# Second expert products two steps behind the first, groups of at most two tiles, and another order of the last jobs, in a two-layer graph network

## The chip, the cores and the metric

The kernel runs on one core of a Trainium2 chip. Its time is the device time of one execution, in microseconds (us). The kernel before takes 2432.77 us, the median of three runs (2429.38 to 2436.04).

## The reference

The network has 3125 nodes with 256 features each and 103125 edges, sorted by destination. It has two layers, and x is carried through both. Cut to what matters here:

```python
xn = layernorm(x)
x = x + edge_conv_max(xn, src, dst) + attention0(xn)          # layer 0
x = x + moe0(layernorm(x))
xn = layernorm(x)                                             # layer 1
h_all = einsum('ni,rio->nro', xn, W)                          # 8 relations
agg = segment_sum(h_all[src, edge_type], dst)
h = gelu(agg + xn @ loop_w + h_bias + xn)
x = x + layernorm(h) * ln_gamma + ln_beta + attention1(xn)
xn = layernorm(layernorm(x)) * gamma + beta                   # experts of layer 1
logits = xn @ Wr + br                                         # the two largest: softmax -> w
for e in range(8):
    y = y + w[:, e] * (gelu(xn @ W1[e] + b1[e]) @ W2[e] + b2[e])    # 256 -> 512 -> 256
x = x + y
```

All eight experts are computed for every node, and w is zero for six of them. Everything is in 32-bit floats. The change lies in layer 1, from `segment_sum` to the end.

## The kernel before, in words

The nodes are sorted by their number of incoming edges and lie in 25 tiles of 128 rows; the last one, tile 24, has 53. The table `STEPS` says how many rows a node of a tile needs at most: 45 for tile 0, 43 for tile 1, 38 for tile 4, 36 for tile 6, 24 for tile 23 and 22 for tile 24. One gather (an indirect DMA issued by POOL, line 195) fetches one row for each of the 128 nodes of a tile, so a tile takes as many gathers as its number in `STEPS`.

**Second layer, gathers.** `edge_pass` (L1336) goes through groups of tiles. The rows of a tile come in chunks of up to four gathers into a buffer `gt` from a pool of five (`gp1`, L2013). DVE adds the rows of a chunk together (L1376) and to the tile's sum `acc` (L1378). A gather into a buffer can start once the additions on the chunk that used it five chunks ago are done. The out rows are scattered by POOL (`flush`, L242) only after the last gather. The groups stand in `GROUPS1` (L67 to 69): tiles (3,4), (1,2), (23,24), (19 to 22), (15 to 18), (12 to 14), (9 to 11), (7,8), (6), (5), (0). The first two pairs have a pass of their own, `first_groups`.

**Second layer, jobs.** When a group's sums are complete, `after1` (L2544) puts its further work into a list `bg` of jobs with costs. After each chunk, `edge_pass` works out a rate, the sum of the costs in `bg` divided by the gathers left in the group, held between 0.9 and 1.3; each gather gives so much credit, and jobs are taken from the list as long as there is credit:

```python
rate = min(max(sum(c for c, _ in bg) / left, pace[0]), pace[1])
credit = min(credit, 0.0) + rate * n1 if bg else 0.0
while bg and credit > 0.0:
    cost, job = bg.popleft()
    job()
    credit -= cost
```

So the order of the program decides which jobs lie between which chunks. DVE and POOL do their work in the order in which it is written; the order on TensorE (PE) and ACT is found by a planner from that.

**A group's jobs** (class `Group`, L2315). *First jobs:* the self loop and attention product (`loops`, L2326 to 2328), the sum and GELU (`gelus`, L2333 to 2335), the two normalizations (`states_a` to `states_d`), the transposes and the routing product (`routes_a`, L2396 and L2404), the choice of the two experts (`routes_b`) and its transposes (`shares`). *Steps:* `step(i)` does three things. `take` (L2489) adds the second products that wait in PSUM to x, on DVE. `hidden(i)` issues the first product of expert i (L2436) and its GELU on ACT (L2441) into a buffer `hT` from the pool `f1` of three. `outputs(i-1)` issues the second product (L2470) of the expert in front, into one of two PSUM banks for each two tiles. There are ten steps, 0 to 9; the last one lets the rows leave. A first product of expert i is called h_i below, a second one o_i, and the product of the weights with the second bias (`constants`) stands ahead of o_0. A group's steps stand in `bg` behind its first jobs, but the last four are kept in `late` and spread among the first jobs of the next group, ahead of `sums_a`, `states_a`, `states_c` and `routes_a` (numbers 0, 3, 5 and 7). Of a pair, all products together lie on PE as h0, h1, constants, o0, h2, o1, h3, and so on to h7, o6, o7.

Of the kernel before, what the change touches and what calls it, by code (L numbers as in the profile page):

```python
# [12 lines left out]
F32 = mybir.dt.float32  # L13
# [8 lines left out]
P = 128  # L22
# [11 lines left out]
NX = 8  # L34
F = 512
FC = F // P
# [27 lines left out]

MADE = tuple(range(1, 25)) + (0,)

CUTS1 = (25, 23, 19, 15, 12, 9, 7, 6, 5)  # L67
PAIRS = ((3, 4), (1, 2))
GROUPS1 = tuple(range(a, b + 1) for a, b in PAIRS) + tuple(range(b, a) for a, b in zip(CUTS1, CUTS1[1:])) + (range(0, 1),)

# [32 lines left out]
def gps_kernel(ctx: ExitStack, tc: tile.TileContext, a, out):  # L103
# [1216 lines left out]
    def fast():  # L1320
# [197 lines left out]
        def hidden(ts):  # L1518
            n, at0 = len(ts) * P, ts[0] * P
            for i in range(2):  # L1520
                if i not in hTs:
                    hTs[i] = f0h.tile([P, FC, 3 * P], F32, name=f"hT0_{i}", bufs=1)
                hT = hTs[i]
                for f in range(FC):
                    ph = ps_mm.tile([P, 512], F32, name="mm")
                    for c in range(2):
                        PE.matmul(  # L1527
                            ph[:, :n], w1[:, i, c, f * P : (f + 1) * P], xT[:, c, at0 : at0 + n],
                            start=(c == 0), stop=(c == 1),
                        )  # L1530
                    S.activation(hT[:, f, :n], ph[:, :n], AF.Gelu, bias=b1[:, i, f : f + 1])
# [57 lines left out]
        with ExitStack() as l0x:  # L1589
# [217 lines left out]
            def mix_weights():  # L1807
                pw = ps_mm.tile([P, 512], F32, name="mm")
                for m in range(2):
                    for c in range(2):  # L1810
                        PE.matmul(
                            pw[:, m * D : (m + 1) * D], w_vT[:, c, m * P : (m + 1) * P], w_o[:, c, :],
                            start=(c == 0), stop=(c == 1),
                        )
                pr = ps_mm.tile([P, 512], F32, name="mm")
                for c in range(2):
                    PE.matmul(pr[0:1, :D], b_v[:, c : c + 1], w_o[:, c, :], start=(c == 0), stop=(c == 1))
                yield
                V.tensor_copy(w_vo, pw.rearrange("p (m d) -> p m d", m=2))
                V.tensor_tensor(b_mix, b_mix, pr[0:1, :D], op=ALU.add)  # L1820
# [26 lines left out]
            class Fin0:  # L1847
# [46 lines left out]
                def jobs(self):  # L1894
                    def step(i):
                        if i < self.k:
                            self.products(i)
                        if i > 0:
                            self.sums(i - 1)

                    out = [(5.0 if 0 < i < self.k else 2.5, lambda i=i: step(i)) for i in range(self.k + 1)]
                    return out + [(2.0 * self.k, self.norms)]

            def staged(gen, costs):
                return [(c, lambda: next(gen, None)) for c in costs]

            bg = deque(staged(mix_weights(), (3.0, 1.0)))
# [277 lines left out]
        with ExitStack() as l1x:  # L2185
# [20 lines left out]
            wf = l1w.tile([P, NT, NX], F32, name="wf")  # L2206

            fin = l1x.enter_context(tc.tile_pool(name="fin1", bufs=1))
            f1 = l1x.enter_context(tc.tile_pool(name="f1", bufs=3))
            wp = l1x.enter_context(tc.tile_pool(name="wp", bufs=1))  # L2210
            w1s, w2s = [None] * NX, [None] * NX

# [99 lines left out]
            class Group:  # L2312
# [114 lines left out]

                def hidden(self, e):
                    n, at0 = self.n, self.at0
                    hT = self.hT[e] = f1.tile([P, FC, 4 * P], F32, name="hT1")  # L2430
                    fs, w = max(4 // self.k, 1), self.k * P
                    for f0 in range(0, FC, fs):
                        ph = ps_mm.tile([P, 512], F32, name="mm")
                        for f in range(f0, min(f0 + fs, FC)):
                            for c in range(2):
                                PE.matmul(  # L2436
                                    ph[:, (f - f0) * w : (f - f0) * w + n], w1s[e][:, c, f * P : (f + 1) * P],
                                    xT[:, c, at0 : at0 + n], start=(c == 0), stop=(c == 1),
                                )
                        for f in range(f0, min(f0 + fs, FC)):  # L2440
                            S.activation(  # L2441
                                hT[:, f, :n], ph[:, (f - f0) * w : (f - f0) * w + n], AF.Gelu, bias=b1[:, e, f : f + 1]
                            )
# [48 lines left out]
                def step(self, i):  # L2492

                    self.take()
                    if i < NX:
                        self.hidden(i)
                    if 1 <= i <= NX:
                        self.outputs(i - 1)
                    if i == NX + 1:
                        leaving.extend(self.tiles)  # L2500

                def jobs(self):
                    k = self.k
                    first = [
                        (2.0, self.sums_a), (2.0, self.sums_b), (1.0, self.sums_c), (1.0, self.states_a),
                        (1.0, self.states_b), (1.0, self.states_c), (1.0, self.states_d), (4.0, self.routes_a),
                        (2.0, self.routes_b), (2.0, self.shares),
                    ]
                    cost = [1.6] + [3.1] * (NX - 1) + [1.6, 0.5]
                    rest = [(c * k, lambda i=i: self.step(i)) for i, c in enumerate(cost)]  # L2510
                    return first, rest

# [15 lines left out]
            bg = deque()  # L2528
# [13 lines left out]
            late = []  # L2542

            def after1(g, tiles, accs):  # L2544

                first, rest = Group(tiles, accs).jobs()
                for i, job in enumerate(first):
                    if late and i in (0, 3, 5, 7):
                        bg.append(late.pop(0))
                    bg.append(job)  # L2550
                bg.extend(rest[:-4])
                late[:] = rest[-4:]
                if g == len(GROUPS1) - 1:
                    bg.extend(late)
# [17 lines left out]
            def first_groups():  # L2572

                credit = 0.0
                load_init(order1[0])
                for g, pair in enumerate(PAIRS):
                    left = sum(STEPS[t] - todo[t] for t in EARLY)
                    while any(todo[t] < STEPS[t] for t in pair):
                        gt = gp.tile([P, 4, D], F32, name="gt")
                        n = 0  # L2580
                        for h in range(2):
                            ts = [t for t in pair if todo[t] < STEPS[t]]
                            for i, t in enumerate(ts):
                                at = U - 1 - STEPS[t] + todo[t]
                                gather(gt[:, 2 * h + i, :], h_rows, idx2[:, t, at : at + 1])
                                todo[t] += 1
                            if ts:
                                e = EARLY.index(ts[0])
                                d = sums[:, e : e + len(ts), :]
                                V.tensor_tensor(d, d, gt[:, 2 * h : 2 * h + len(ts), :], op=ALU.add)  # L2590
                            n += len(ts)
                        rate = min(max(sum(c for c, _ in bg) / left, 0.9), 2.0)
                        left -= n
                        credit = min(credit, 0.0) + rate * n if bg else 0.0
# [4 lines that stand above are left out]
                    after1(g, pair, [sums[:, EARLY.index(t), :] for t in pair])  # L2599

            with tc.manual_schedule(engines={mybir.EngineType.DVE, mybir.EngineType.Pool}):
                first_groups()
                edge_pass(
                    gp, h_rows, D, lambda t: idx2[:, t, :], ALU.add, bg, lambda g, *a: after1(g + 2, *a),
                    GROUPS1[2:], 4, (0.9, 1.3), lambda t: inits[t], begin1, lambda: None,
                )
                while bg:
                    bg.popleft()[1]()
                    flush()
# [3 lines left out]
    with tc.If(unfit < 1):  # L2613
        fast()
# [78 lines left out]
```

## Time and profile before

| | us |
|---|---|
| median of three runs | 2432.77 (2429.38 to 2436.04) |
| the profiled execution | 2431.52 |
| its span | 2429.8 |
| last gather of the second layer issued | 2344.28 |
| first expert product of tile 0, the last group | 2388.08 |
| PE, POOL, DVE, ACT busy | 1689.2, 1705.9, 1236.6, 532.4 |
| mean clock granted to TensorE | 0.832 of full speed |

The profile is of one execution. Its times are counted from the span's start. A group of instructions is given by its line, its engine, and the names of what it writes and reads. "Waits" lists, for each engine and operation, what ended the idle time before it: total us, how many times, and the longest. "issue" there is time in which the engine waited for nothing that the profile shows. In a timeline each line has the start, the duration, the engine, line and operation, the names and shapes, how many instructions it joins, and in brackets the idle time in front with its releaser.

### The profile page before, as it was taken

How to read it: one execution, taken by the hardware profiler on the slowest of the kernel's cores; microseconds unless marked ns; L12 is line 12 of the kernel's file. 1: busy time of each engine (PE TensorE's matmuls, PEld its weight loads, DVE VectorE, ACT ScalarE, POOL GpSimd, SP SyncE). 2: the span in 40 equal slices, each digit the busy share in tenths (PEclk: the TensorE clock that was granted, in tenths of full speed). 3: DMA queues.
4: the chain of work that ended last, by engine and by line, in shares of the span. 5: the costliest groups of instructions: out<-in, count | busy, mean ns of one | idle time of the engine just before them, and what ended most of it. 6: DMA issues, size and time to landing. Idle time of an engine off the chain costs nothing.

```text
span 2429.8 us, 20895 instructions
## 1 busy us (share of the span) xinstructions
PE 1689.2 (70%) x6033; PEld 1106.3 (46%) x6033; DVE 1236.6 (51%) x3393; ACT 532.4 (22%) x1263; POOL 1705.9 (70%) x1847
## 2 busy tenths in 40 slices
PE   3446697502946526267699836988687899989997
PEld 2323344301624313145344324766354566667786
DVE  7655555525534434344567435554543636465542
ACT  4313231001201101012222222322211222132343
POOL 4577777777777777777126777677777777777771
PEclk9777887855978667687799977998798999999999
DMA  6544434344444344444156754333333333333330
GB/s 197 146 109 110 110 105 129 105 108 137 108 107 107 105 109 106 108 105 107 58 186 240 268 166 149 94 104 103 108 101 110 104 104 110 107 103 103 102 101 19
DMA packets 124809, 289.03 MB, mean 119 GB/s; under 512 B 41258, under 2 KB 62830, under 8 KB 121480
## 3 DMA queue, kind: packets, MB, share of 16 engines
q0 software_dynamic: 83184, 230.02, 34.3%
q1 hardware_dynamic: 36970, 54.83, 6.7%
q10 hardware_dynamic: 4526, 2.71, 0.4%
q8 instruction: 51, 0.84, 0.1%
q14 instruction: 78, 0.64, 0.1%
HBM read 248.54 MB, written 38.89 MB: 118 GB/s over the span
## 4 chain that ended last, share of the span: by engine, by line
PE 23%; POOL 9%; issue 8%; DVE 5%; DMA 4%; ACT 1%; DVEq 0%; POOLq 0%; ACTq 0%
POOL gt L195 8%; PE mm L2436 7%; PE py L2470 7%; PE mm L190 7%; DMA gt<-htab_f,idx2g 3%; DVE gt L1376 1%; POOL out_dram L242 1%; DVE bnst L164 1%; PE pt L2404 1%; PE mm L2328 1%; PE mm L2326 0%; DVE x L2369 0%; DVE acc L1378 0%; DVE x L2489 0%; DVE hh L2368 0%
## 5 line engine op out<-in xcount | busy, mean ns | idle before, releaser
L195 POOL DMA_INDIRECT gt<-btab,idx x764 | 742.9, 972 | 232.7 <-issue 193.4
L195 POOL DMA_INDIRECT gt<-htab_f,idx2g x718 | 704.2, 981 | 225.0 <-issue 192.5
L1369 DVE TENSOR_TENSOR run<-run,gt 128x512 f32<-128x512 f32 (+1 forms) x400 | 266.9, 667 | 470.7 <-DMA gt<-btab,idx 468.9
L2470 PE MATMUL py<-w,hT 128*128 128x256 f32 (+1 forms) x1600 | 376.8, 391 | 46.4 <-DVE x L2489 46.4
L2436 PE MATMUL mm<-xT,w 128*128 128x256 f32 (+4 forms) x1408 | 377.1, 422 | 5.9 <-DVE x L2334 5.9
L2470 PEld LDWEIGHTS py<-w,hT 128*128 128x128 f32 (+1 forms) x1600 | 305.4, 194 | 111.8 <-DVE x L2489 26.4
L2436 PEld LDWEIGHTS mm<-xT,w 128*128 128x128 f32 x1408 | 249.4, 203 | 109.3 <-issue 68.1
L1376 DVE TENSOR_TENSOR gt<-gt 128x512 f32<-128x512 f32 (+1 forms) x344 | 182.6, 531 | 175.3 <-DMA gt<-htab_f,idx2g 168.9
L2441 ACT ACTIVATE hT<-mm,b 128x256 f32<-128x256 f32 (+4 forms) x352 | 158.5, 493 | 393.9 <-PE mm L2436 393.7
L190 PE MATMUL pt<-w_own,xT 128*128 128x256 f32 x100 | 38.8, 524 | 265.9 <-DVE acc L1869 265.9
L190 PE MATMUL mm<-w_rel,xT 128*128 128x512 f32 x400 | 175.0, 595 | 3.5 <-ACT xT L185 3.5
L2489 DVE SCALAR_TENSOR_TENSOR x<-py,wf,x 128x256 f32<-128x256 f32 x200 | 87.1, 477 | 143.8 <-PE py L2470 143.8
L190 PEld LDWEIGHTS pt<-w_own,xT 128*128 128x128 f32 x100 | 23.8, 261 | 277.2 <-DVE acc L1869 270.9
L195 POOL DMA_INDIRECT gt<-htab_f,soon x96 | 93.5, 974 | 53.3 <-issue 20.1
L190 PEld LDWEIGHTS mm<-w_rel,xT 128*128 128x128 f32 x400 | 74.9, 190 | 95.8 <-issue 84.2
L1527 PE MATMUL mm<-xT,w 128*128 128x384 f32 (+2 forms) x320 | 96.8, 468 | 16.2 <-DMA w<-in_f_W_dram 16.2
L190 PE MATMUL mm<-w_qkv,xT 128*128 128x512 f32 (+1 forms) x200 | 90.5, 564 | 19.0 <-ACT vs L1775 18.5
L1876 ACT ACTIVATE rs<-rs 128x3 f32<-128x3 f32 (+2 forms) x11 | 2.2, 203 | 446.1 <-DVE rs L1875 446.1
L1556 PE MATMUL mm<-w,hT 128*128 128x256 f32 x400 | 97.5, 399 | 0.0
L1887 PE MATMUL pmean<-ones,xt 128*128 128x1 f32 (+1 forms) x100 | 21.2, 315 | 105.8 <-DVE xt L173 105.8
L1556 PEld LDWEIGHTS mm<-w,hT 128*128 128x128 f32 x400 | 77.1, 198 | 30.8 <-issue 20.5
L1527 PEld LDWEIGHTS mm<-xT,w 128*128 128x128 f32 x320 | 64.2, 221 | 48.3 <-DMA w<-in_f_W_dram 14.9
(441 smaller groups left out, 2214.7 us busy)
## 6 DMA issues: line engine op xcount, KB each, us to landing
htab_f<-hs SPq DMA_DIRECT2D x25, 1024.0 KB
gt<-btab,idx POOLq DMA_INDIRECT x764, 2.8
gt<-htab_f,idx2g POOLq DMA_INDIRECT x718, 2.8
w<-in_f_W_dram SPq DMA_DIRECT2D x20, 512.0 KB
ntab<-x SPq DMA_DIRECT2D x5, 640.0 KB
btab<-bs SPq DMA_DIRECT2D x5, 640.0 KB
x<-in_x_dram SPq DMA_DIRECT2D x4, 640.0 KB
otab<-xn SPq DMA_DIRECT2D x12, 128.0 KB
```

Of the source, the lines that this page charges most:

```text
L164: V.bn_stats(out=st, in_=src)
L190: PE.matmul(ps, lhs[:, c, t * P : (t + 1) * P], w[:, c, :], start=start and c == 0, stop=stop and c == 1)
L195: G.indirect_dma_start(out=dst, out_offset=None, in_=table, in_offset=bass.IndirectOffsetOnAxis(ap=idx, axis=0))
L242: G.indirect_dma_start(out=table, out_offset=bass.IndirectOffsetOnAxis(ap=idx, axis=0), in_=src, in_offset=None)
L1369: V.tensor_tensor(d, d, gt[:, k1 - b : k1 - a, :], op=op)
L1376: V.tensor_tensor(gt[:, :h, :], gt[:, :h, :], gt[:, m - h : m, :], op=op)
L1527: PE.matmul(ph[:, :n], w1[:, i, c, f * P : (f + 1) * P], xT[:, c, at0 : at0 + n], start=(c == 0), stop=(c == 1),)
L1556: PE.matmul(py[:, i * D : (i + 1) * D], hTs[i][:, f, j * P : (j + 1) * P], w2[:, i, f, :], start=False, stop=(f == FC - 1), skip_group_che ...
L2436: PE.matmul(ph[:, (f - f0) * w : (f - f0) * w + n], w1s[e][:, c, f * P : (f + 1) * P], xT[:, c, at0 : at0 + n], start=(c == 0), stop=(c == 1),
L2441: S.activation(hT[:, f, :n], ph[:, (f - f0) * w : (f - f0) * w + n], AF.Gelu, bias=b1[:, e, f : f + 1])
L2470: PE.matmul(py[:r, j * D : (j + 1) * D], hT[:, f, at : at + r], w2s[e][:, f, :], start=(f == 0), stop=(f == FC - 1),)
L2489: V.scalar_tensor_tensor(d, y, wf[:r, t, e : e + 1], d, op0=ALU.mult, op1=ALU.add)
```

## The change

Three things are changed together.

1. `step(i)` issues `outputs(i-2)` in place of `outputs(i-1)`: a second product stands two steps behind its first. A group has eleven steps in place of ten, with the costs moved accordingly, and a fourth buffer `hT` holds the hidden values that wait.
2. `CUTS1` cuts the tiles from 22 down to 9 into pairs: (21,22), (19,20), (17,18), (15,16), (13,14), (11,12), (9,10) take the place of (19 to 22), (15 to 18), (12 to 14), (9 to 11). The groups in front of these and behind them stay. As no group has more than two tiles, a buffer `hT` is half as large.
3. For the last group (tile 0) `after1` takes all jobs that are still in `bg`, that is, the steps of tile 5 that aren't done when tile 0's gathers end, puts them ahead of the late ones, and places one of them ahead of each of tile 0's first jobs; what is left goes behind the first jobs. In all other groups the last four steps are spread as before; there are eleven steps now, so these are the steps 7 to 10 (o5 with h7, o6, o7, and the leaving of the rows).

On PE a pair's products then lie as h0, h1, constants, h2, o0, h3, o1, and so on to h7, o5, o6, o7, and the next group's `loops` come between o5 and o6.

```diff
-CUTS1 = (25, 23, 19, 15, 12, 9, 7, 6, 5)
+CUTS1 = (25, 23, 21, 19, 17, 15, 13, 11, 9, 7, 6, 5)
...
-            f1 = l1x.enter_context(tc.tile_pool(name="f1", bufs=3))
+            f1 = l1x.enter_context(tc.tile_pool(name="f1", bufs=4))
...
-                    hT = self.hT[e] = f1.tile([P, FC, 4 * P], F32, name="hT1")
+                    hT = self.hT[e] = f1.tile([P, FC, 2 * P], F32, name="hT1")
...
                     self.take()
                     if i < NX:
                         self.hidden(i)
-                    if 1 <= i <= NX:
-                        self.outputs(i - 1)
-                    if i == NX + 1:
+                    if 2 <= i <= NX + 1:
+                        self.outputs(i - 2)
+                    if i == NX + 2:
                         leaving.extend(self.tiles)
...
-                    cost = [1.6] + [3.1] * (NX - 1) + [1.6, 0.5]
+                    cost = [1.6, 1.6] + [3.1] * (NX - 2) + [1.6, 1.6, 0.5]
...
             def after1(g, tiles, accs):
 
                 first, rest = Group(tiles, accs).jobs()
+                if g == len(GROUPS1) - 1:
+                    late[:0] = bg
+                    bg.clear()
                 for i, job in enumerate(first):
-                    if late and i in (0, 3, 5, 7):
+                    if late and (i in (0, 3, 5, 7) or g == len(GROUPS1) - 1 and i):
                         bg.append(late.pop(0))
                     bg.append(job)
+                bg.extend(late)
                 bg.extend(rest[:-4])
                 late[:] = rest[-4:]
                 if g == len(GROUPS1) - 1:
                     bg.extend(late)
```

## The prediction

> **What bounds the kernel now.** I read the page first, for the engines' shares and the gathers.
>
> ```profile
> span 2429.8 us, 20895 instructions
> ...
> PE 1689.2 (70%) x6033; PEld 1106.3 (46%) x6033; DVE 1236.6 (51%) x3393; ACT 532.4 (22%) x1263; POOL 1705.9 (70%) x1847
> ...
> L195 POOL DMA_INDIRECT gt<-htab_f,idx2g x718 | 704.2, 981 | 225.0 <-issue 192.5
> ```
>
> A gather of the second layer keeps POOL 0.98 us and the next starts 0.30 us later; by POOL's timeline 78 start in each 100 us from 1600 to 2300, 1.28 us each. Then who POOL waits for, from 1480 to 1600 (first) and from 1600 to 2344:
>
> ```profile
> POOL gt L195 <- DVE acc L1378: 8.5, 7, 3.7
> ```
>
> ```profile
> POOL gt L195 <- issue: 156.6, 514, 0.3
> POOL gt L195 <- DVE gt L1376: 4.9, 16, 0.3
> POOL gt L195 <- DVE acc L1378: 4.3, 14, 0.3
> ```
>
> From 1600 on no wait is over the 0.3 us of issue: POOL alone sets the pace of the second layer's gathers. Before 1600 there are three longer waits for an addition on DVE (1.02, 3.72 and 2.50 us), 6.3 us above 0.3. There DVE was held by TensorE, and the five gather buffers were full. The timeline of PE over that pair's turn:
>
> ```profile
> 1543.18 1.02 PE L2326 MATMUL mm<-w_lu,xT 128*128 128x512 f32 x2
> ...
> 1548.26 3.62 PE L2436 MATMUL mm<-xT,w 128*128 128x256 f32 x16
> 1551.71 7.07 PE L2470 MATMUL py<-w,hT 128*128 128x256 f32 x32
> 1562.38 1.23 PE L2396 MATMUL pt<-ident,hh 128*128 128x128 f32 x4 [3.60 <-DVE hh L173]
> ...
> 1564.29 1.20 PE L2436 MATMUL mm<-xT,w 128*128 128x256 f32 x2
> ...
> 1566.42 8.22 PE L2436 MATMUL mm<-xT,w 128*128 128x256 f32 x26
> ...
> 1576.71 3.72 PE L2470 MATMUL py<-w,hT 128*128 128x256 f32 x16
> ```
>
> A product of a pair (first or second) takes 3.45 us from start to start, and no second product waits for its GELU. Only the first jobs (loops at 1543.18 to transposes at 1562.38, 19.2 us of DVE) leave a hole, 3.60 us, although one first and two second products (10.4 us) lie in it. The end, by the timelines of POOL and PE:
>
> ```profile
> 2344.28 1.13 POOL L195 DMA_INDIRECT gt<-htab_f,idx2g  x1 [0.30 <-issue]
> ```
>
> ```profile
> 2347.91 0.66 PE L2396 MATMUL pt<-ident,hh 128*128 128x128 f32 x2 [5.38 <-DVE hh L173]
> ```
>
> ```profile
> 2386.78 0.47 PE L2396 MATMUL pt<-ident,hh 128*128 128x128 f32 x2 [3.71 <-DVE hh L173]
> ...
> 2388.08 1.20 PE L2436 MATMUL mm<-xT,w 128*128 128x128 f32 x4
> ```
>
> The last gather is issued at 2344.28; tile 0's first product starts 43.8 us later, behind tile 5's, and the span ends 41.7 us after that. The profiled execution took 2431.52 us, 1.72 outside its span; the median of three is 2432.77. I work out a displacement and add it to the median.
>
> **The change, part by part.** *Two steps behind.* The extra hT buffer and the delay free the second products of a wait that the timeline does not show: no gain. Each group gets one step more, but no product more. What moves is the cover of the first jobs: the last four steps, spread among the next group's first jobs, held one first and three second products, and now hold one first product ahead of the loops and, between loops and transposes, only two second ones. So 3.45 us of cover leave each pair's hole. The DVE chain shortens too: in the old stretch it had one 3-row chunk of additions more (1.25 us, 1549.92 to 1551.17). The hole grows from 3.6 to about 6.0 us. A pair's turn on a fully loaded TensorE, second product of expert 0 to the next group's, was 71.6 us (1505.10 to 1576.71); it becomes 71.6+3.45-1.25, about 73.8. The first delay also puts expert 2's first product ahead of the first o_0, 3.45 us once.
>
> *Pairs instead of fours and threes.* Products and loops cost the same per tile (first product 6.87 us in fours, 3.45 in pairs). But three more groups mean three more holes, and the pacing now stays at its cap (1.3 units a gather) from tile 23 to tile 15, where before it was there for tiles 23 and 24 alone: a pair's jobs cost 68 units, tiles 21 and 22 have 51 gathers. Running the pacing lines through gives which job follows which chunk: just ahead of tile 23's first chunk stands the wait for o_0 of tiles 3 and 4, just behind the fifth of tile 16 that for o_0 of tiles 17 and 18, five turns later. On TensorE these take 5 x 73.8 = 369, less 8 x 0.89 for tile 24's 53 rows (2.56 us a first product instead of 3.45), plus one more chunk in one chain (1.25) and L1398 (0.65): 364 us. As many gathers took from 1489.7 to 1836.9 in the old profile, 347 us, 341 without the waits. POOL can be five chunks ahead, and is at both ends (about 22 us), so it waits for the difference: 23 us instead of 6.3, +17. In the next turn three chunks lie in the chain and TensorE still needs as long as the gathers: I add 1. From tile 11 on a turn has 65 to 72 gathers (83 to 92 us) against 75; nothing waits, and what was lost stays lost: the last gather is 18 us later. Bounds: a turn as measured (71.6) is 2.2 less six times, +5; the whole 3.45 without the saved chunk (75.1) is 1.3 more six times, +26. I take 18: it is nearest to the rows of this pair's own chain.
>
> The other added work has cover: three groups' small operations on DVE (about 15 us, DVE 51% busy), table loads on ACT (nine of 1.28 us, ACT 22%), PSUM and weights unchanged. The smaller hT buffers free memory and move no transfer; the out rows and own-row gathers on POOL are as many as before.
>
> *The last tiles.* At 1.28 us a gather, tile 6's first chunk ends 147 us ahead of the last gather. Old: tiles 7 and 8's first product starts 49 us behind that chunk (2246). New: their first jobs follow the tile's first five chunks, so it starts 28 us behind it (in that chain DVE sets the time: the fourth chunk's additions end at 23.1, a take and states c and d at 25.8, transposes and routing add 1.9), 21 us ahead. From there TensorE is the slower engine and loses most of that. Tiles 7, 8 to tile 6: 19.6 to the end of o_0 (16.1 above plus 3.45), 34.5 for ten products, 13.4 from loops to transposes (additions 3.4, two chunks 3.0, two takes 1.6, four state jobs 5.4), 1.2 = 69 us, old 62.8. Tile 6 to 5 likewise 12.3+17.5+12.8+1.3 = 44, old 40.5. Tile 5 to 0: 12.3, then 23.5 for twelve products and loops, and 4.5 for the last take, two states and transposes = 40.4, old 38.8: here all that is left of tile 5 lies among tile 0's first jobs, and a hole of about 3 us stays (old 3.71), because states b, c and d stand behind takes that wait for the last second products. 28+69+44+40.4 = 181: tile 0's first product starts 34 us after the last gather instead of 43.8, -10. What follows has the same order: 41.7. Bounds: only the last hole goes, -3.7; nothing of tile 5 is left when the gathers end, -25 (then only 5.1 us from the last gather's issue to its addition and 13.2 of chain, 2374.9 to 2388.08, stand before tile 0's first product, 18.3 instead of 43.8). I take -10, between them, because tile 5's products are counted above row by row and some of them must be left.
>
> Sum: +18-10 = +8, 2441 us. Changes under 0.3% (7.3 us) I count as none, about what a measurement of this kernel can tell.
>
> The row on the clock: after the 3.60 us hole 26 records took 8.22 us (0.32 each) where 16 take 3.62 (0.22), 2.6 us lost; after 10.38 us the loss was about 2.8. I leave it unchanged per hole; three more holes on TensorE's path are in the turns. [...]
>
> **Rivals.** *The tail wins* (faster). If TensorE is not the bound between tiles 21 and 15, because the hole is closed by products running ahead, a turn is at most 71.6, the last gather is late by 0 to 5, and the end gains 10 to 15: 2423 us. For it: lagging steps let TensorE run a step ahead, and from 1900 it was 95% busy without holding POOL up. Against it: the order on TensorE puts nothing between the second product of expert 7 and the transposes. It decides at a turn of about 72.5: below, the sum is under zero.
> *Both cancel*: turn 72.5 to 73.3, shift 9 to 14, end -10: within 7 us of before, 2434.
> *TensorE falls further behind*: a turn of 75, or the end gains only 3.7: +14 to +22, 2452. For it: in POOL's stretches TensorE waited 46.4 us for `take` and 32.7 for hh, and more groups mean more such places.
> *The delay does nothing*: argued above; it is part of every case, since no wait for GELU is there to remove.
>
> **How the numbers follow.** Forecast (turn 73.4 to 74.6, net +5 to +14) 0.48, of it 0.14 under 7.3; tail wins 0.22, of it 0.03 within; cancel 0.14, of it 0.01 faster; further behind 0.16. Faster 0.20, same 0.30, slower 0.50. The range leaves out the outer half of the two outer rivals: 2423 to 2454; the forecast's own is 2437 to 2447.
>
> **What would show it.** Right: POOL waits for DVE acc L1378 of 20 us and more between 1530 and 1930; holes of about 6 us before the pairs' transposes; last gather at about 2362; tile 0's first product 34 us behind it. Wrong: no waits of POOL after 1600 (the turn stays under 72.5), or tile 0's first product 25 us after the last gather (TensorE not late at the end).

## The result, and the profile after

The changed kernel takes 2443.01 us (median of eight runs, 2438.5 to 2447.97). The kernel before takes 2431.97 us in its eight runs. The ratio is 1.0048 with a 95% interval of 1.0038 to 1.0059: 11 us slower. The forecast was 2441 (against 2432.77, +8) with a range of 2423 to 2454.

The profiled execution of the changed kernel is its slowest of the eight, 2447.97 us with a span of 2446.3. Of the 16.5 us between the two profiled spans, 4.7 lie ahead of the change: the first of the 718 gathers in the row below starts at 1405.93 before and at 1410.66 after, and nothing that runs ahead of it was edited. So distances within each profile are compared below, not times from the span's start.

From the page of the changed kernel:

```profile
span 2446.3 us, 21869 instructions
...
PE 1722.4 (70%) x6417; PEld 1201.0 (49%) x6417; DVE 1249.1 (51%) x3467; ACT 563.7 (23%) x1391; POOL 1710.1 (70%) x1847
...
L195 POOL DMA_INDIRECT gt<-htab_f,idx2g x718 | 704.4, 981 | 250.0 <-issue 188.8
```

The 718 gathers are as long as before (704.4 against 704.2 us). The idle time in front of them was 225.0 and is 250.0: POOL stands still 25.0 us more. Who it waits for, from 1480 to 1600 (first) and from 1600 to 2370:

```profile
POOL gt L195 <- DVE acc L1378: 14.1, 6, 5.2
POOL gt L195 <- DVE rsh L2380: 1.6, 1, 1.6
```

```profile
POOL gt L195 <- DVE acc L1378: 20.4, 21, 4.8
POOL gt L195 <- DVE rsh L2380: 4.0, 1, 4.0
```

From 1600 on, the kernel before had no wait over the 0.3 us of issue. Now there are waits of up to 4.8 us. By POOL's timeline 14 waits are longer than 0.5 us, the last at 1947.87; above the 0.3 us of issue they come to 31.15 us, against 6.34 before. That is +24.8, and the gathers of the second layer, first to last, take 963.33 us (1410.66 to 2373.99) against 938.35, which is +25.0. So nearly the whole delay of the last gather is in these waits.

Why DVE is late is in PE's timeline, over the same pair as before (tiles 1 and 2 behind tiles 3 and 4):

```profile
1550.92 1.02 PE L2326 MATMUL mm<-w_lu,xT 128*128 128x512 f32 x2
...
1555.99 7.07 PE L2470 MATMUL py<-w,hT 128*128 128x256 f32 x32
1568.57 1.22 PE L2396 MATMUL pt<-ident,hh 128*128 128x128 f32 x4 [5.51 <-DVE hh L173]
...
1572.60 7.34 PE L2436 MATMUL mm<-xT,w 128*128 128x256 f32 x26
...
1585.85 3.62 PE L2470 MATMUL py<-w,hT 128*128 128x256 f32 x16
```

Between the loops and the transposes two second products are left (7.07 us), and the hole in front of the transposes is 5.51 us (3.60 before). The same hole stands in every later turn of a pair up to tiles 9 and 10, 5.5 to 8.3 us. From one o_0 to the next a turn takes 72.92, 72.96, 69.86 (here tile 24 has its 53 rows), 74.11, 74.76, 75.55, 75.74 and 74.92 us, where the old pair took 71.62. (The o_0 of tiles 23 and 24 is counted from 1658.81, where 14 of its 16 instructions start; two run ahead at 1653.81.) PE's waits from 1500 to 2350 show the exchange:

```profile
PE pt L2396 <- DVE hh L173: 67.5, 11, 8.3
PE py L2470 <- DVE x L2489: 12.7, 4, 6.0
```

For the kernel before the same two rows are 38.1 us in 5 waits and 46.4 us in 12: waits for `take`, which its groups of four and three had, have mostly gone, and waits for the transposes' input have come, eleven in place of five.

The end, by the timelines of POOL and of PE:

```profile
2373.99 0.95 POOL L195 DMA_INDIRECT gt<-htab_f,idx2g  x1 [0.30 <-issue]
```

```profile
2386.39 1.02 PE L2326 MATMUL mm<-w_lu,xT 128*128 128x512 f32 x2
...
2402.66 0.66 PE L2396 MATMUL pt<-ident,hh 128*128 128x128 f32 x2 [3.09 <-DVE hh L173]
...
2404.10 1.20 PE L2436 MATMUL mm<-xT,w 128*128 128x128 f32 x4
```

Tile 0's first product starts 30.1 us behind the last gather (43.8 before, -13.7). From there to the span's end it is 42.2 us (41.7). The sum is +25.0 - 13.7 + 0.5 = +11.8 us, and the medians differ by 11.0.

### The profile page after: what moved, and what is told of

Same layout as the page of the kernel before. It is cut to its first block, busy times and chain, and to the rows that moved or that the text cites. A ratio compares the mean times of both kernels' runs of the same rounds, so it can differ in the third digit from the quotient of the medians.

```text
span 2446.3 us, 21869 instructions
## 1 busy us (share of the span) xinstructions
PE 1722.4 (70%) x6417; PEld 1201.0 (49%) x6417; DVE 1249.1 (51%) x3467; ACT 563.7 (23%) x1391; POOL 1710.1 (70%) x1847
## 4 chain that ended last, share of the span: by engine, by line
PE 28%; POOL 7%; DVE 6%; issue 6%; DMA 3%; ACT 1%; DVEq 0%; POOLq 0%; ACTq 0%
PE mm L2436 11%; PE py L2470 7%; PE mm L190 6%; POOL gt L195 6%; DMA gt<-htab_f,idx2g 2%; DVE gt L1376 2%; POOL out_dram L242 1%; PE pt L2404 1%; DMA gt<-htab_f,soon 1%; DVE x L2489 1%; DVE bnst L164 1%; PE mm L2328 1%; DVE acc L1378 1%; PE mm L2326 0%; PE py L2456 0%
## 5 line engine op out<-in xcount | busy, mean ns | idle before, releaser
L195 POOL DMA_INDIRECT gt<-htab_f,idx2g x718 | 704.4, 981 | 250.0 <-issue 188.8
L2436 PE MATMUL mm<-xT,w 128*128 128x256 f32 (+2 forms) x1792 | 399.5, 379 | 0.2 <-ACT hT L2441 0.2
L2470 PE MATMUL py<-w,hT 128*128 128x256 f32 (+1 forms) x1600 | 369.2, 384 | 13.8 <-DVE x L2489 13.8
L2436 PEld LDWEIGHTS mm<-xT,w 128*128 128x128 f32 x1792 | 332.7, 207 | 46.1 <-issue 7.2
L2470 PEld LDWEIGHTS py<-w,hT 128*128 128x128 f32 (+1 forms) x1600 | 300.8, 190 | 68.7 <-issue 23.8
L2441 ACT ACTIVATE hT<-mm,b 128x256 f32<-128x256 f32 (+2 forms) x448 | 170.7, 440 | 345.7 <-PE mm L2436 345.4
L190 PEld LDWEIGHTS pt<-w_own,xT 128*128 128x128 f32 x100 | 24.8, 272 | 273.7 <-DVE acc L1869 266.6
L1527 PE MATMUL mm<-xT,w 128*128 128x384 f32 (+2 forms) x320 | 96.7, 468 | 17.7 <-DMA w<-in_f_W_dram 17.7
L190 PE MATMUL mm<-w_qkv,xT 128*128 128x512 f32 (+1 forms) x200 | 95.9, 594 | 18.5 <-ACT vs L1775 18.0
L1556 PEld LDWEIGHTS mm<-w,hT 128*128 128x128 f32 x400 | 76.8, 197 | 30.6 <-issue 20.5
L1527 PEld LDWEIGHTS mm<-xT,w 128*128 128x128 f32 x320 | 64.3, 222 | 49.6 <-DMA w<-in_f_W_dram 15.5
```

The source lines that it names most:

```text
L190: PE.matmul(ps, lhs[:, c, t * P : (t + 1) * P], w[:, c, :], start=start and c == 0, stop=stop and c == 1)
L195: G.indirect_dma_start(out=dst, out_offset=None, in_=table, in_offset=bass.IndirectOffsetOnAxis(ap=idx, axis=0))
L1527: PE.matmul(ph[:, :n], w1[:, i, c, f * P : (f + 1) * P], xT[:, c, at0 : at0 + n], start=(c == 0), stop=(c == 1),)
L1556: PE.matmul(py[:, i * D : (i + 1) * D], hTs[i][:, f, j * P : (j + 1) * P], w2[:, i, f, :], start=False, stop=(f == FC - 1), skip_group_che ...
L2436: PE.matmul(ph[:, (f - f0) * w : (f - f0) * w + n], w1s[e][:, c, f * P : (f + 1) * P], xT[:, c, at0 : at0 + n], start=(c == 0), stop=(c == 1),
L2441: S.activation(hT[:, f, :n], ph[:, (f - f0) * w : (f - f0) * w + n], AF.Gelu, bias=b1[:, e, f : f + 1])
```

## The experiments

All of these runs fell on chips on which every kernel, the kernel before too, took 2912 to 3034 us, some 23% more than in the result. The profile shows how: ACT, DVE and PE stop again and again in a way that it can't put down to any instruction ("remote" or "issue"), which no engine did for over 1 us between 1550 and 2350 us of the first two profiles. The kernel before, run as an experiment of its own on such a chip, shows it in its waits between 1800 and 2840 (first DVE's row, then ACT's):

> The kernel before itself, for its profile on the chips of these runs and for how far two series of one kernel differ: a ratio of 0.996 to 1.004. If the pauses that the profile doesn't name sit in all kernels alike: POOL's long waits together 240 to 290 us, as in the runs so far, and some waits of second products for their GELU (hT), 5 to 30 us, of which its first profile has none.

```profile
DVE x L2489 <- remote: 160.7, 13, 21.7
```

```profile
ACT hT L2441 <- remote: 206.3, 22, 28.7
```

POOL's long waits (over 0.5 us, counted above the 0.3 us of issue) come to 259.3 us in the second layer instead of 6.3. And against itself this kernel measured 0.9934 (0.9911 to 0.9958), an interval that leaves out 1. So a difference of 0.7% between two series on these chips decides nothing, and no time below settles a question of 0.5%. What the runs can settle is what a single stretch of a trace shows where no pause falls into it.

### The cover of the first jobs: three, four and five late steps, one and two steps behind

Three edits change which products lie between a pair's loops and its transposes.

```diff
-                bg.extend(rest[:-4])
-                late[:] = rest[-4:]
+                bg.extend(rest[:-5])       # three late steps: -3 in both lines
+                late[:] = rest[-5:]
```

> The changed kernel with five late steps instead of four (rest[-5:]), so that one more first and one more second product lie among the next group's first jobs, 13.8 us of products between loops and transposes instead of 6.9. If the missing cover makes the turn long: holes of 0 to 2.5 us before the transposes instead of 5.5 to 8.3, turns of 67 to 70 us instead of 73 to 76, long waits of POOL under 8 us, last gather within 4 us of before, and a time of 2420 to 2430. Rival, DVE's chain or the pace of the jobs sets the turn: the hole shrinks but DVE holds POOL up as long as before, waits of 25 us or more, and 2438 or more.

> The changed kernel with five late steps again, since in the first series every engine lost time that the kernel before doesn't lose in its profile (the kernel before took 2986.93 us there). If that was a matter of the chip or the hour, the kernel before is at 2432 again. Then, if the missing cover makes the turn long: holes of 0 to 2.5 us before the transposes, turns of 67 to 70 us, long waits of POOL under 8 us, a time of 2420 to 2430. Rival, DVE's chain or the pace of the jobs sets the turn: waits of 25 us or more, and 2438 or more.

> The changed kernel with three late steps instead of four (rest[-3:]): one second product less lies between loops and transposes, 3.45 us of cover instead of 6.9. If the hole is the first jobs' chain less its cover: the shortest holes before the pairs' transposes 8 to 10 us, after 5.3 with four late steps and none with five, and a ratio 0.003 to 0.008 above the changed kernel's 0.995. Rival, TensorE's pauses take the hole in: holes as expected, but a ratio within 0.003 of the changed kernel's.

The third is the changed kernel one step behind (pairs and the new order of the last jobs stay; the costs, the three buffers `hT` and their old size come back with it):

```diff
-                    if 2 <= i <= NX + 1:
-                        self.outputs(i - 2)
+                    if 1 <= i <= NX:
+                        self.outputs(i - 1)
...
```

> The changed kernel one step behind instead of two (three buffers hT; pairs and the new order of the last jobs stay). If the lag only uncovers the hole: shortest holes 3.3 to 3.8 us instead of 5.3, and a ratio at or below the changed kernel's 0.995. Rival, where ACT is late by pauses of its own the second step saves waits for GELU: waits of L2470 for hT of 8 to 20 us as in the other kernels one step behind, none in those two steps behind, and a ratio of 0.999 to 1.005, above the changed kernel's.

> The changed kernel one step behind, again, beside the last one. The hole of the first pair after tiles 1 to 4 is 3.6 us (5.5 two steps behind). If the chips are as in the result: turns of 71 to 72.5 us between tiles 21 and 15 instead of 72.9 to 75.5, POOL's long waits together 12 to 22 us instead of 31, and 2428 to 2438. Rival, the pairs alone set the turn: waits of 28 us or more and 2440 or more. If the kernel before takes 2950 or more: waits for GELU of 8 to 20 us, and a ratio that says nothing within 0.7%.

The first turn after tiles 3 and 4 is free of pauses between loops and transposes in nearly all of these traces. PE's timelines: three late steps, then four (the changed kernel itself on such a chip), then one step behind.

```profile
1883.32 3.62 PE L2470 MATMUL py<-w,hT 128*128 128x256 f32 x16
1896.08 1.23 PE L2396 MATMUL pt<-ident,hh 128*128 128x128 f32 x4 [9.14 <-DVE hh L173]
```

```profile
1862.31 7.07 PE L2470 MATMUL py<-w,hT 128*128 128x256 f32 x32
1874.88 1.23 PE L2396 MATMUL pt<-ident,hh 128*128 128x128 f32 x4 [5.50 <-DVE hh L173]
```

```profile
1862.74 3.62 PE L2436 MATMUL mm<-xT,w 128*128 128x256 f32 x16
1866.19 7.07 PE L2470 MATMUL py<-w,hT 128*128 128x256 f32 x32
1876.88 1.22 PE L2396 MATMUL pt<-ident,hh 128*128 128x128 f32 x4 [3.62 <-DVE rsh L2387]
```

| | products between loops and transposes | hole of the first turn, us |
|---|---|---|
| three late steps | o7 | 9.14 |
| four (the changed kernel) | o6, o7 | 5.50 |
| one step behind | h7, o6, o7 | 3.62 (3.63 in the second run) |
| five late steps | h7, o5, o6, o7 | none |

With one product less the hole is 3.64 us longer, a product's 3.45 and a little. With one product more, in the kernel one step behind, it is only 1.88 shorter, since DVE's chain there has the chunk more that the prediction spoke of: loops to transposes take 19.22 us (1857.66 to 1876.88) instead of 17.65 (1857.23 to 1874.88). With five late steps no turn of a pair has a hole in front of its transposes, in either run. So the hole is the chain of the first jobs less the products that cover it. Two steps behind with four late steps takes one of them away.

But the five late steps did not buy a turn. In the place of the hole stands another wait, for PSUM: `take` now lies among the first jobs on DVE, and the last second product has no bank until it is done. PE's row of waits from 1800 to 3010, first of the second run with five late steps, then of the changed kernel:

```profile
PE py L2470 <- DVE x L2489: 60.7, 9, 23.8
```

```profile
PE py L2470 <- DVE x L2489: 2.9, 2, 2.4
```

In the pairs' turns of that run these waits are 2.2 to 9.8 us each; the longest, 23.8, lies at the end, among tile 5's first jobs. The ratios to the kernel before are 1.0069 (1.0028 to 1.0111) and 1.0088 (1.0054 to 1.0121); three late steps gave 1.0011 (0.9965 to 1.0058), one step behind 0.9982 (0.995 to 1.0013) and 0.9983 (0.9955 to 1.0011). Five late steps are the only kernel above 1 in two series, so as a repair they are not supported. On the forecasts: the holes of the first turn came as expected everywhere. The ratios that were forecast differ by less than what these chips move for no change, so none of them is decided; one step behind came between its two (0.995 and below, 0.999 and above). Turns of 67 to 72 us and POOL's waits could not be read (the turns of the pairs are 79 us and longer in these runs), and "under 8 us" or "12 to 22 us" of waits were missed by far, 275 to 297 us, as in all kernels on these chips.

### What the second step of delay is good for

> The changed kernel itself, beside the kernel before, as the measure for the runs so far, in which the kernel before took 2950 to 2990 instead of 2432. If the kernel before takes 2432 here: ratio 1.003 to 1.006, as in the result. If it takes 2950 to 2990: my reading is that what the added holes cost is hidden there, because TensorE stops anyway for reasons that the profile doesn't name, so a ratio of 0.995 to 1.003, near that of the kernel without the new order of the last jobs (0.9989). Rival, the holes add to those stops: 1.004 or more.

The ratio was 0.9951 (0.9912 to 0.999), within what the kernel before gave against itself. But one row separates the kernels cleanly. Waits of second products for their GELU, by PE's waits from 1800 to 3010, in the kernel before (first) and in the changed kernel with one step (second):

```profile
PE py L2470 <- ACT hT L2441: 10.1, 3, 8.7
```

```profile
PE py L2470 <- ACT hT L2441: 9.9, 4, 5.3
```

The six traces with one step on these chips all have such waits, 17.8, 9.8, 10.1, 9.9, 9.4 and 12.8 us, where the first profile of the kernel before has none. Of the six two steps behind, five have none and one has 3.0 us (three late steps). So the second step does what it says where ACT stops unforeseen. On the chip of the result ACT doesn't, and there is nothing to win.

### The pairs alone, and the changed kernel with the old order of the last jobs

> The kernel before with the pairs alone (one step behind, old order of the last jobs). If the length of a turn is set by the hole of the first jobs, which the lag uncovers by 3.45 us: holes before the transposes of 2 to 4 us as in the old pair's row (3.60), turns of 70 to 71.6 us, POOL's long waits together 6 to 16 us instead of 31, tile 0's first product about 30 us behind the last gather, and 2420 to 2428. Rival, the pairs alone send more jobs per gather than TensorE can do, whatever the hole: long waits of 28 us or more, and 2440 or more.

> The changed kernel with the old order of the last jobs (pairs, two steps behind). The last gather is as late as in the changed kernel, with long waits of POOL of 28 to 34 us. If the new order of the last jobs brings little: within 3 us of the changed kernel, 2440 to 2446. Rival, it brings the 13.7 us: 2452 or more.

The first is the kernel before with the new `CUTS1`, the second the changed kernel with the old body of the loop over `first`:

```diff
-                if g == len(GROUPS1) - 1:
-                    late[:0] = bg
-                    bg.clear()
...
-                    if late and (i in (0, 3, 5, 7) or g == len(GROUPS1) - 1 and i):
+                    if late and i in (0, 3, 5, 7):
...
-                bg.extend(late)
```

The pairs alone gave 1.004 (1.0002 to 1.0078) with a first hole of 3.72 us; the old order gave 0.9989 (0.9956 to 1.0021) with a first hole of 5.51 us. The holes follow the delay, as in the table; the times decide nothing. POOL's long waits (282.3 and 268.9 us) are those of the pauses, so both forecasts of them were missed.

### The new order of the last jobs alone

The kernel before with only the change in `after1`:

> The kernel before with the new order of the last jobs alone (groups of four and three, one step behind). If the tail's gain of 13.7 us comes from the pairs, whose products start earlier relative to the last gather: the last gather stays where it was (2344 from a table that is complete at about 1406), tile 0's first product stays 42 to 46 us behind it, and the time is within 3 us of before, 2432. Rival, the order itself brings the gain: tile 0's first product comes 30 to 36 us behind the last gather, and the time is 8 us or more below before.

> The kernel before with the new order of the last jobs alone, again, since the kernel before measured against itself differed by 0.7% on these chips. In the stretch from tile 5's first second product to the end of TensorE's work, which is nearly free of pauses in the runs so far: 52 to 54 us and no hole before tile 0's transposes, as in its first run (52.5), where the kernel before has 62 to 64 with a hole of 3.71 and the changed kernel 61.6 to 62.1 with 3.09. If the chips are as in the result (the kernel before at 2432): 2421 to 2428, a ratio of 0.996 to 0.998, and tile 0's first product 34 to 38 us behind the last gather instead of 43.8. Rival, the shorter stretch is paid back ahead of it: 2430 or more.

Here the traces say more than I expected. The stretch from tile 5's transposes to PE's end has almost no pauses in these runs (in the two traces below no idle time of PE in it is over 0.5 us but the holes in front of the transposes). PE's timelines there, first the kernel before (tile 5's transposes, tile 0's loops, tile 0's transposes), then the new order alone, where tile 0's loops come first:

```profile
2884.40 0.41 PE L2396 MATMUL pt<-ident,hh 128*128 128x128 f32 x2 [2.63 <-DVE hh L173]
...
2911.23 1.02 PE L2326 MATMUL mm<-w_lu,xT 128*128 128x512 f32 x2
...
2915.55 3.62 PE L2470 MATMUL py<-w,hT 128*128 128x256 f32 x16
2922.89 0.41 PE L2396 MATMUL pt<-ident,hh 128*128 128x128 f32 x2 [3.71 <-DVE hh L173]
```

```profile
2897.72 1.02 PE L2326 MATMUL mm<-w_lu,xT 128*128 128x512 f32 x2
...
2902.20 0.41 PE L2396 MATMUL pt<-ident,hh 128*128 128x128 f32 x2 [1.79 <-DVE hh L173]
...
2928.68 1.89 PE L2470 MATMUL py<-w,hT 128*128 128x256 f32 x8
2930.41 0.38 PE L2396 MATMUL pt<-ident,hh 128*128 128x128 f32 x2
```

In the kernel before, 11.7 us lie between tile 0's loops and its transposes, with a hole of 3.71. With the new order 32.7 us lie between them, filled with tile 5's products, and there is no hole. From tile 5's o_0 to PE's end, the stretch that the second expectation names, it takes 62.4 us in the kernel before on these chips (63.7 in its first profile), 52.5 and 54.2 in the two runs of the new order alone, and 61.6 and 62.2 in the two profiles of the changed kernel, which has the same new order but a hole of 3.09. But that mark doesn't stand at the same work everywhere: with the new order alone some products of tile 5 and the loops of tile 0 are already done at it. Tile 5's transposes are a better mark. From them to PE's end it takes 70.7 us in the kernel before on these chips (72.4 in its first profile), 63.9 and 64.0 with the new order alone, and 72.7 in the first profile of the changed kernel. Of the 70.7 us, 2.5 are tile 0's loops, which the new order moves ahead of the stretch, so what is won in it is about 4.2 us in both runs. The reason for the difference between the two kernels with the new order is how much of tile 5 is still in `bg` when tile 0's gathers end. With the old groups tile 0's loops come ahead of tile 5's transposes, so all products of tile 5 are left to hide tile 0's chain. With the pairs tile 5 is further on: in the changed kernel's profile tile 0's loops come 12.3 us behind tile 5's o_0 (2374.12 to 2386.39), and what is left is not enough. It is the pairs that do this and not the second step: the changed kernel one step behind has such a hole too, 2.76 us in both runs.

The expectation of the first run (no gain) was wrong at this place. Of its rival only the direction is shown: tile 0's first product comes 78.9 and 74.3 us behind the last gather (83.3 in the kernel before on these chips), with pauses in all three, so its figures could not be read. Nor is it settled whether the shorter stretch is paid back ahead of it, as the rival of the second expectation says: from the last gather's issue to PE's end, with the pauses, it takes 114.4 and 109.8 us against 114.5. What it is worth for the whole kernel I could not measure: the ratios are 0.9987 (0.9951 to 1.0023) and 0.9938 (0.9906 to 0.997), and the kernel before gave 0.9934 against itself.

### A lower rate of jobs

The changed kernel with a cap of 1.2 units a gather:

```diff
-                    GROUPS1[2:], 4, (0.9, 1.3), lambda t: inits[t], begin1, lambda: None,
+                    GROUPS1[2:], 4, (0.9, 1.2), lambda t: inits[t], begin1, lambda: None,
```

> The changed kernel with the cap of the jobs' rate at 1.2 units a gather instead of 1.3: a pair's 68 units then lie among 57 gathers (73 us at 1.28) instead of 52 (67 us), which is what a turn of TensorE takes (73 to 76 us). If POOL waits because the jobs are written ahead of what TensorE can do, where a turn is longer than the gathers it lies among: on chips where the kernel before takes 2432, long waits of POOL of 5 to 15 us instead of 31, turns unchanged at 73 to 76, last gather 15 to 25 us earlier relative to the table, part of it given back at the end since more work is left over: 2428 to 2438. Rival, the waits come from DVE's chain within the first jobs, wherever they lie: waits of 25 us or more and a time within 3 us of the changed kernel. If all engines lose time as in the first series (the kernel before near 2970), it tells nothing of the two.

1.0015 (0.9965 to 1.0065), POOL's long waits 254.9 us: the pauses cover the question, as the expectation's last sentence says, and it stays open. The end agrees with what was said of the new order. More work is left over at the end of the gathers, tile 0's transposes have no hole, and from tile 5's transposes to PE's end it is 65.2 us, tile 0's loops included, where the changed kernel took 72.7 in its first profile.

## Why the prediction was right, point by point

**The sign and the size.** +8 forecast, +11 measured. Both terms were larger than forecast: the gathers +25.0 instead of +18, the end -13.7 instead of -10. The errors, +7.0 and -3.7, have opposite signs, so that the sum came nearer than its first term did is luck.

**No wait for the delay to remove.** Right for the chip of the result: the profile of the changed kernel has no gain from it. That it does remove waits elsewhere, the runs showed.

**The hole.** Forecast about 6.0 us (the terms given for it, 3.60 + 3.45 - 1.25, make 5.8), measured 5.51 in the pair for which it was worked out, since the chain from loops to transposes is 17.65 us (19.20 before), 1.55 shorter where 1.25 was taken off. That the missing product makes the hole is shown by the table of covers.

**The turn.** 73.8 forecast, 72.92 measured for that pair. From o_0 of tiles 3 and 4 to that of tiles 17 and 18, five turns, the forecast was 364 us; it is 364.6 (1512.93 to 1877.54). Later turns were longer than 73.8 (up to 75.74, with holes of up to 8.3 us), which the forecast did not have.

**POOL's waits.** Up to the end of the fifth turn the waits above the 0.3 us of issue are 25.6 us, 19.3 more than before; 17 was forecast, 2.3 less. Most of these 2.3 us seem to come from the start: DVE's first addition to tile 23's sum (L1378) comes 24.0 us behind the last gather of tiles 1 to 4 and came 21.5 us behind it before. That fits the delay of the first o_0 ("3.45 us once"), which the prediction names and leaves out of the sum of the five turns. Behind the fifth turn the waits are 5.5 us, where the prediction said "I add 1". This is the step that was mis-sized most, and with the 2.3 us in front of it nearly the whole error of +7.0. The reason given there, that TensorE needs as long as the gathers, holds, but a turn of 75.55 us came where about 74 was reckoned, and POOL was still at the end of its five buffers. From 1948 on nothing waits, as forecast.

**The end.** The transposes of tiles 7 and 8 lie 121.6 us ahead of the last gather, against 101.1: 20.5 us earlier, 21 forecast. TensorE then loses part of it, as forecast: from those transposes to tile 0's it takes 150.3 us against 143.6. The three turns of 69, 44 and 40.4 us are 69.4, 41.3 and 39.7, from transposes to transposes. The turn from tile 6 to 5 was mis-sized by 2.7 us, most of the 3.7 by which the end was better. The hole of about 3 us that the prediction left in front of tile 0's transposes is 3.09. One reading was off without entering the sum: the old start of tiles 7 and 8's first product is 2244.43, not 2246, so the old turn to tile 6 is 64.3 us, not 62.8.

**The clock.** The prediction left the loss per hole as it was. From the transposes to the first o_0 or h_2 behind them, the granted clock (the third figure from the end of the row, ahead of the DMA share and GB/s) was, before and after:

```profile
1562.38:1576.71 14.33, 14.10 (x50) 11.12 (x50) 6.58 (x23) 7.84 (x14) 9.25 (x10) 0.69 0.32 92
```

```profile
1568.57:1582.30 13.73, 13.38 (x51) 10.47 (x51) 6.54 (x23) 7.66 (x14) 6.92 (x7) 0.74 0.25 68
```

After the longer hole it is not lower (0.74 against 0.69), and 26 records took 7.34 us instead of 8.22. In the later turns, apart from tile 24's, the 26 records took 7.61 to 8.88 us, and not by the length of the hole: 8.88 after 6.06 us, 7.77 after 8.32. So the longer holes give no reason to raise the loss per hole. What sets it is not shown by these traces.

**The rivals.** "The tail wins" was to decide at a turn of 72.5 and below; the turns are 72.9 and above (but for the 69.86 with tile 24's 53 rows), so it fell by the row that it named, though narrowly in the first two turns. These two lie within the 72.5 to 73.3 of "both cancel", but the shift was 25.0 us where that rival has 9 to 14. "TensorE falls further behind" had the nearer shift (its upper bound was +26, measured +25.0), but took too little for what the end gains.

**What stays open.** One part of the gathers' delay can be told apart in the profiles of the two kernels, one of each. Up to the end of tile 24's gathers the groups are the same in both kernels, pairs, and for five chunks more a gather waits only for additions that were written before that end. So in this stretch only the delay, with its costs and its buffer, differs. It holds all three long waits of the kernel before (to 1575.62, 6.3 us above the issue) and the first five of the changed kernel (to 1581.44, 13.5 us). So 7.1 of the 24.8 us come with the second step alone. The other 17.7 us fall where the old groups of four and three have become pairs, and how they divide between the longer holes, the added ones and the pacing could not be measured: the chips of the experiments move by 0.7% for no change of the kernel. That the uncovered product makes the hole is shown. That the hole makes POOL wait was followed through the profile of the result, turn by turn, and not by a run that takes it away there. What one step of delay, a lower cap or the old groups would save of the 11 us stays open too.

## What to carry to other kernels

Delaying a product by a step takes it out of the place where it stood: before you do it, look for what the product covered there, and count the hole that it leaves, once for every group. A deeper pipeline takes waits away where the producer is late (on the chips of the experiments 9.4 to 17.8 us of them with one step, none in five of six traces with two), so look for a wait on the producer first; without one it only costs cover (a hole of 5.51 us in place of 3.60). And an order that hides the last chain among what is left needs something to be left: speeding up the tile in front takes the cover away that the new order was to use (a hole of 3.09 us with the pairs, none with the old groups).

## What the runs showed of the hardware that was not expected

On the chips of the experiments the same kernel took 2912 to 3017 us in place of 2432. The mean granted clock is lower (0.765 in its profile there, 0.832 in the first), but the instructions that no pause falls into keep their pace: a gather still takes 0.98 us on average (0.977, 0.982 and 0.978 by POOL's timelines of the second run of the new order alone and of the two runs one step behind; 0.981 in the first profile), and a pair's product that no pause falls into 3.62 us. What is added are pauses of ACT, DVE and PE (one of ACT's lasted 28.7 us) that the profile gives no cause for, while POOL has next to none of its own: by the same three timelines, of the 718 gathers one in each of the first two waits over 0.6 us for "issue" (1.52 and 1.56 us), and none in the third. A hole in front of the transposes and such a pause behind them may stand for each other, which is not shown: in the second run with five late steps, where the hole is gone, PE stopped for 3.5 to 8.5 us behind the transposes (L2404) in eight of ten turns of the pairs, and in the changed kernel on such a chip for 2.5 to 7.6 us in five of ten. The first turn of the second run with five late steps, by PE's timeline:

```profile
1861.07 0.60 PE L2396 MATMUL pt<-ident,hh 128*128 128x128 f32 x4
1868.76 0.60 PE L2404 MATMUL pt<-wr,xT 128*128 128x8 f32 x2 [7.08 <-issue]
```

What stops the engines there was not found.
